# A written order on five engines for the last turn of a two-layer graph kernel, with the end by row blocks

## The chip, the cores and the metric

The kernel runs on one core of a Trainium2 chip. The metric is the device time of one execution in microseconds (us); the figure for a kernel is the median of several executions. The engines are TensorE (PE, matrix products), VectorE (DVE), ScalarE (ACT), GpSimd (POOL) and SyncE (SP, which issues the DMAs here).

## The reference

The input is 64 graphs of 256 nodes with 256 features, and a 0/1 adjacency matrix for each graph. Two layers follow each other, all in float32.

```
layer 0:  h = gat(gat(x, adj, W1, a1), adj, W2, a2)        # softmax over one axis of leaky_relu scores
          h = layernorm(x + h) * g_ln1 + b_ln1
          x = layernorm(h + relu(h @ w_ff1 + b_ff1) @ w_ff2 + b_ff2) * g_ln2 + b_ln2
layer 1:  q, k = x @ Wq + bq, x @ Wk + bk                  # 8 heads of 32
          attn = softmax(q k^T / sqrt(32))
          out  = sum over r of (attn * (adj == r)) @ (x @ Wv[r] + bv[r])     # adj has 0 and 1 only
          x    = layernorm(x + out @ Wo + bo) * g1 + beta1
          out  = layernorm(x + gelu(x @ W1 + b1) @ W2 + b2) * g2 + beta2
```

The hidden width of both feed-forward parts is 1024.

## The kernel before

**Tiling.** Two graphs (G = 2) are worked on together as a pair `u`. There are 32 pairs (NG). A pair's activations `y` are T = 4 row blocks of 128 rows by 256 features; the first NB = 2 blocks are graph 0 of the pair, the other two are graph 1. A layer norm takes, for each row block, statistics on DVE (`bn_stats`, `bn_aggr`, L842 and L843), the inverse deviation on POOL (`rs`, an add and a power, L853 and L854), an offset `nm` on DVE (`offsets`, L861), and one ACT instruction that applies both (`applied_norm`, L871). The gain and the shift of the norm come later as two DVE passes over all four blocks (`affine` = `times` L880 and `plus` L883, 128x1024 elements each). `rg2`/`rb2`, `rg3`/`rb3` and `rg4`/`rb4` are gain and shift of the second norm of layer 0 and of the two norms of layer 1.

**Stages.** A turn `turn(y_, x_, z)` (L1238) works on three pairs: the attention and the feed-forward part of layer 1 for pair `y_`, the feed-forward part of layer 0 for the next pair, and the attention layers of layer 0 for the pair after that. PE works through the stages without a gap in the middle of the run, since each stage's waits are covered by products of another pair. In turn 30 there is no third pair left, in turn 31 neither a second nor a third.

**The pieces of a turn's layer 1.** `Projections` computes queries, keys and values with seven half-size products each (steps q1 to q7 and v1 to v7). It reads the features transposed, with a row of ones that carries the bias; POOL writes that row (`with_ones`, memset L692). `scores(n)`, n = 0 to 3, are the products for one graph and one half of the heads, with their exponentials on ACT (`powers`); `masks(n)` multiplies by the adjacency and `totals(n)` sums pairs, both on DVE. `sums(n)` gives the weighted values (`po`) and the row sums (`zo`) on PE. `shares(b)` is a chain on DVE that divides graph b: transpose of `zo`, reciprocal, transpose, multiply (L1131, L1132, L1138, L1140). It empties the PSUM bank of `po`. `out_(b)` is the output projection `yop` and its addition to y (L827, L830).

**The feed-forward part.** `hidden_seven` (L885) gives the hidden layer with seven products in place of eight; step names are a digit and a half, "7a" for example, and the letters c, d and s stand for activations alone. Each product goes to a PSUM bank, which ACT copies (L927) or DVE adds (L924) into the hidden features. Four differences of the transposed features (L897) are made on DVE first. `HiddenOut` (L974) is the way back to 256 features, again with seven products, taken in the order 1, 2, 5, 6, 3, 7, 4. Products 1, 6, 7 and 4 share one bank, and 5 and 3 another; `add` (L1012) adds a product to one half of a graph's y, and `sums` (L990) forms the four sums of the hidden features.

**The order of the work.** The instructions are written in one Python program for all engines, and a scheduler in the framework arranges each engine's queue by its own priorities. Inside `tc.manual_schedule(engines=...)` the named engines keep the written order. The outer loop names PE and SP. A turn names PE, SP, DVE and ACT, but turn 31 names only PE and SP (`[:4 if X else 2]`), so its work on DVE, ACT and POOL is placed by the scheduler. A framework rule adds semaphore waits wherever one engine reads or overwrites what another still uses.

**Turns 30 and 31.** The feed-forward output of pair 30 is not done in its own turn. `out_pieces` (L1196) is a generator that holds its seven products, and `piece()` (L1234) lets turn 31 run the next one between its scores. `finish` (L1216) norms one graph, applies rg4 and rb4 and issues the store of that graph, 256 KB. In turn 31 the affine steps of pair 30 (rg3, rb3) and pair 31 (rg2, rb2) are done by DVE, from the list `late`. Pair 29's last affine step (rg4, rb4) and store lie in turn 30 (L1520 to L1522). The program ends with a check: sums of values gathered on the way (`low`, `lowg`, `high`, `other`), a one-column product, and the flag `bad` (L1711 to L1720), which SP loads and all engines branch on (L1729).

Of the kernel before, what the change touches and what calls it, by code (L numbers as in the profile page):

```python
# [385 lines left out]
def narrow_path(  # L386
# [498 lines left out]
    def hidden_seven(u, l, hT, w, bi, func, d, tt):  # L885
# [13 lines left out]
        sub(0, quarter[0][1], quarter[0][0])  # L899
        sub(1, quarter[1][1], moving(0))  # L900
        sub(2, quarter[1][1], quarter[0][1])
        sub(3, quarter[1][0], moving(1))
# [68 lines left out]

        return steps

    class HiddenOut:  # L974
# [17 lines left out]
        def product(s, n):  # L992
# [4 lines left out]
            for old, new in ((1, 6), (6, 7), (7, 4), (5, 3)):  # L997
                if n == new:
                    s.ps[n] = s.ps[old]
            a, w_ = {1: (s.a[0], b11), 2: (s.a[1], b21), 5: (s.s[0], t1), 6: (s.s[1], t2),  # L1000
                     3: (s.s[3], b22), 7: (s.s[2], t3), 4: (s.a[3], t4)}[n]
            for i in range(NB):
                for k in range(K2):
                    nc.tensor.matmul(s.ps[n][:, i * F2:(i + 1) * F2], a[:, k, i * P:(i + 1) * P], w_[:, k, :],  # L1004
                                     start=n in (1, 2, 5) and i == 0 and k == 0, stop=True,
                                     skip_group_check=True)

        def add(s, n):
            b, o = {1: (0, 0), 2: (0, 0), 5: (1, 1), 6: (0, 1), 3: (0, 1), 7: (1, 1), 4: (1, 0)}[n]
            F2 = F // 2  # L1010
            yq = s.y[:, b * NB:(b + 1) * NB, o * F2:(o + 1) * F2]
            mark["out"] = nc.vector.tensor_tensor(yq, s.ps[n][:, :F].rearrange("p (i f) -> p i f", i=NB), yq, ALU.add)  # L1012
# [183 lines left out]
    def out_pieces(u, y, h1):  # L1196

        if u == NG - 2:
            s = [io.tile([P, T, N], F32, tag="y", name=f"sq{u}", bufs=4),
                 work.tile([P, T, WX], F32, tag="wh", name=f"wq{u}")[:, :, :N]]  # L1200
            s += [io.tile([P, T, N], F32, tag=t, name=f"sq{u}_{t}", bufs=1) for t in ("xq", "aq")]
        else:
            s = out_sums(u, 1)
        end = HiddenOut(u, 1, y, h1, w2s, s)
        end.sums(1, 2, 4, 3)
        for n, p in enumerate((1, 2, 5, 6, 3, 7, 4)):
            end(p)
            if n in (4, 6):
                finish(u, y, n // 6)
            yield  # L1210
# [5 lines left out]
    def finish(u, y, b):  # L1216

        normed(u, 3, y, range(b * NB, (b + 1) * NB))
        bt = slice(b * NB, (b + 1) * NB)
        affine(y[:, bt, :], rg4, rb4)  # L1220
        stored(u, y, bt)
# [11 lines left out]

    def piece():  # L1234
        if left:
            next(left[0], None)

    def turn(y_, x_, z):  # L1238
# [43 lines left out]
        def moved(moves, n):  # L1282
            for _ in range(n):
                nc.scalar.copy(*next(moves))

        order = tc.manual_schedule(engines={getattr(mybir.EngineType, n) for n in
                                            ("PE", "SP", "DVE", "Activation")[:4 if X else 2]})
        with order:
# [29 lines left out]
            if X:  # L1318
# [58 lines left out]
                totals(3)  # L1377
                sums(2)
                sums(3)
                first("4b")  # L1380
            else:
                powers(0, (1,))
                p("q3 v3")
                powers(0, (2, 3))
                p("q6 v6 q7 v7")
                with behind("projected"):
                    masks(0)
                    totals(0)
                while late:
                    affine(*late.pop(0))  # L1390
                p("q4 v4")
                scores(1)
                masks(1)
                totals(1)
                sums(0)
                piece()
                scores(2)
                sums(1)
                piece()
                with behind("out"):  # L1400
                    shares(0)
                masks(2)
                totals(2)
                scores(3)
                piece()
                piece()
                masks(3)
                totals(3)
                sums(2)
                sums(3)  # L1410
# [13 lines left out]
            piece()  # L1424
# [9 lines left out]
            piece()  # L1434
# [21 lines left out]
            elif X:  # L1456
                out.product(5)
                out.sums(3)
                out.add(5)
            if X and not Z:  # L1460
                out(6)
# [11 lines left out]
            elif X:  # L1473
                out.sums(4)
                out(7, 3)
            if not Z:
                piece()
                hT = to_features(y, f"h3T{y_}")
                hT = [h.rearrange("p (t a r) -> p t a r", t=T, r=32) for h in hT]
                if not X:  # L1480
                    affine(y, rg3, rb3)
# [33 lines left out]
            else:  # L1515
# [4 lines left out]
                if waiting:  # L1520
                    affine(waiting[0][1], rg4, rb4)
                    stored(*waiting.pop(), slice(0, T))  # L1522
                if X:
                    offsets(*n)
                    applied_norm(X["y"], *n, [0])
                second("3a")
# [3 lines left out]
                if X:  # L1530
                    applied_norm(X["y"], *n, [2, 3], True)
                second("6a 6b ca cb da db 7a 7b")
# [3 lines left out]
            if y_ >= NG - 2:  # L1536
                pieces = out_pieces(y_, y, h1)
                if X:
                    left.append(pieces)
                    late.append((y, rg3, rb3))  # L1540
                    late.append((X["y"], rg2, rb2))
                else:
                    for _ in pieces:
                        pass
# [216 lines left out]
```

## Time and profile before

| what | us |
|---|---|
| median of 3 executions (all three alike) | 2962.51 |
| the profiled execution | 2958.02 |
| span in its profile | 2956.4 |
| PE busy | 2923.1 (99%) |
| DVE busy | 2607.3 (88%) |
| ACT busy | 1902.0 (64%) |
| POOL busy | 628.2 (21%) |

Times in the profile run from the start of the span. Turn 30's attention ends near 2838, turn 31's projections start at 2869.78, its last output products at 2931.34, and the span ends at 2956.4. A row of the timeline gives start, duration, engine, line, operation, the written and the read tiles with their shapes, a count if several are joined, and the idle time of that engine before it with what ended the wait. A row of the windows gives the stretch, its length, the busy time of PE, PEld, DVE, ACT and POOL with their instructions, the clock that PE was granted (1.00 is full), and the DMA figures.

### The profile page before, as it was taken

The page shows a single profiled execution, that of the slowest core. Times are in us where ns is not written, and L with a number is a line of the kernel's source. Part 1 is how long each engine was busy: PE and PEld are TensorE (multiplying, and loading weights), DVE is VectorE, ACT ScalarE, POOL GpSimd, SP SyncE. Part 2 cuts the span into 40 slices and gives each one's busy share as a digit, 9 for nine tenths or more (in the row PEclk, how much of TensorE's full clock was granted, in tenths as well). Part 3 has the DMA queues.
Part 4 walks back from the last instruction along what each step waited for, and adds up shares of the span by engine and source line. Part 5 has one row for each costly group of instructions (what it writes and reads, how often), then busy time and mean ns, then how long its engine had stood idle before and what let it go on. Part 6 is the DMA issues. An engine that isn't in the chain of part 4 may idle for free.

```text
span 2956.4 us, 58614 instructions
## 1 busy us (share of the span) xinstructions
PE 2923.1 (99%) x22192; PEld 2504.0 (85%) x22192; DVE 2607.3 (88%) x5023; ACT 1902.0 (64%) x3990; POOL 628.2 (21%) x930
## 2 busy tenths in 40 slices
PE   8999999999999999999999999999999999999998
PEld 6788888888888888888888888888888888888876
DVE  5788899889999888999889898989998889988987
ACT  5476676676666666766766666666667667667653
POOL 4222121122221221211221211221112212112211
PEclk9999999999999999999999999999999999999999
DMA  5011111111111111111111111111111111111000
GB/s 152 11 32 32 37 30 28 31 35 37 34 30 23 39 32 37 32 30 28 39 32 37 28 24 38 32 38 32 33 24 39 32 37 30 29 32 32 18 8 16
DMA packets 407955, 99.27 MB, mean 34 GB/s; under 512 B 357770, under 2 KB 407156, under 8 KB 407668
## 3 DMA queue, kind: packets, MB, share of 16 engines
q1 hardware_dynamic: 406268, 94.13, 14.7%
q8 instruction: 178, 2.92, 0.4%
q0 software_dynamic: 1056, 1.05, 0.1%
q14 instruction: 109, 0.89, 0.1%
q10 hardware_dynamic: 344, 0.28, 0.0%
HBM read 56.78 MB, written 16.78 MB: 25 GB/s over the span
## 4 chain that ended last, share of the span: by engine, by line
PE 96%; DVE 2%; ACT 1%; POOL 1%; issue 0%; DMA 0%; ACTq 0%; POOLq 0%; DVEq 0%
PE yf L1004 26%; PE h1a L915 15%; PE h1b L915 11%; PE po L1120 8%; PE qk L1071 6%; PE v L1071 6%; PE sp L1092 4%; PE hpp L816 4%; PE xpp L755 4%; PE yop L827 4%; PE ygp L827 4%; PE zo L1123 2%; PE rows L764 1%; ACT y L871 0%; DVE st L842 0%
## 5 line engine op out<-in xcount | busy, mean ns | idle before, releaser
L1101 ACT ACTIVATE e<-sp 128x512 f32<-128x512 f32 x512 | 271.1, 612 | 71.2 <-issue 43.8
L1105 DVE TENSOR_TENSOR ea<-e,aT 128x1024 f32<-128x1024 f32 x256 | 310.2, 1213 | 1.6 <-ACT e L1101 1.6
L871 ACT ACTIVATE y<-y,nm,rs 128x256 f32<-128x256 f32 x450 | 239.5, 591 | 84.4 <-DVE nm L861 79.4
L924 DVE TENSOR_TENSOR h<-h1a,h 128x512 f32<-128x512 f32 x293 | 197.0, 680 | 83.7 <-PE h1a L915 80.9
L927 ACT COPY h<-h1b 128x512 f32<-128x512 f32 x293 | 175.3, 599 | 124.3 <-PE h1b L915 122.5
L933 ACT ACTIVATE h<-h,cols 128x256 f32<-128x256 f32 x512 | 221.9, 502 | 35.8 <-DVE h L924 31.6
L717 POOL COPY hT<-yt 32x256 f32<-32x256 f32 x244 | 211.2, 866 | 146.5 <-DVE yt L700 135.4
L1058 ACT COPY qk<-qk 128x512 f32<-128x512 f32 x128 | 74.3, 581 | 240.7 <-PE qk L1071 240.0
L853 POOL TENSOR_SCALAR rs<-mv 128x4 f32<-128x4 f32 (+1 forms) x134 | 42.7, 319 | 813.7 <-DVE mv L843 440.2
L1012 DVE TENSOR_TENSOR y<-yf,y 128x256 f32<-128x256 f32 x448 | 184.9, 413 | 34.3 <-PE yf L1004 34.2
L842 DVE BATCH_NORM_STATS2 st<-y 128x6 f32<-128x256 f32 x512 | 208.5, 408 | 5.6
L933 ACT ACTIVATE h<-h1a,cols 128x256 f32<-128x256 f32 x256 | 102.5, 465 | 132.0 <-PE h1a L915 132.0
L1133 POOL TENSOR_TENSOR low<-low,rq 128x16 f32<-128x16 f32 x64 | 13.9, 217 | 813.1 <-DVE rq L1132 813.1
L883 DVE TENSOR_TENSOR y<-y,rb 128x1024 f32<-128x1024 f32 (+1 forms) x130 | 166.1, 1278 | 2.3
L880 DVE TENSOR_TENSOR y<-y,rg 128x1024 f32<-128x1024 f32 (+1 forms) x130 | 155.6, 1197 | 1.2 <-ACT y L871 1.1
L1110 DVE TENSOR_TENSOR es<-e 128x1024 f32<-128x1024 f32 x128 | 155.4, 1214 | 0.0
L854 POOL TENSOR_TENSOR rs<-rs,mhalf 128x4 f32<-128x4 f32 (+1 forms) x134 | 139.8, 1044 | 8.4
L1092 PE MATMUL sp<-qk 32*128 32x256 f32 x2048 | 137.9, 394 | 0.0
L915 PE MATMUL h1a<-tt,wf 128*128 128x256 f32 x512 | 137.7, 392 | 0.0
L1120 PE MATMUL po<-e,v 128*32 128x256 f32 x2048 | 135.5, 382 | 0.0
L1120 PE MATMUL po<-ea,v 128*32 128x256 f32 x2048 | 134.4, 379 | 0.0
L700 DVE STREAM_TRANSPOSE yt<-y 128x256 f32<-128x256 f32 x364 | 128.1, 407 | 0.6 <-ACT y L871 0.6
(280 smaller groups left out, 7721.0 us busy)
## 6 DMA issues: line engine op xcount, KB each, us to landing
hT<-yt SPq DMA_DIRECT2D x666, 32.0 KB, 1.9
y<-in_x_dram SPq DMA_DIRECT2D x32, 512.0 KB, 4.8
xq<-in_x_dram SPq DMA_DIRECT2D x240, 64.0 KB, 2.2
aq<-in_adj_dram SPq DMA_DIRECT2D x240, 64.0 KB, 2.4
out_dram<-y SPq DMA_DIRECT2D x30, 512.0 KB
wf<-in_L_gnn_w_ff_dram SPq DMA_DIRECT2D x2, 1024.0 KB, 7.2
w<-in_L_gnn_W_dram SPq DMA_DIRECT2D x2, 1024.0 KB, 8.2
first<-in_adj_dram POOLq DMA_DIRECT2D x2, 512.0 KB, 7.9
```

The lines of the kernel that those rows point to most:

```text
L717: nc.gpsimd.tensor_copy(to, at)
L827: nc.tensor.matmul(ps[:, i * F:(i + 1) * F], lhs(t, k), rhs(b, k), start=(k == 0), stop=(k == n - 1))
L842: nc.vector.bn_stats(st[:, t, :], y[:, t, :])
L871: mark["normed"] = nc.scalar.activation(y[:, t, :], y[:, t, :], AF.Identity, bias=nm[:, t:t + 1], scale=rs[:, t:t + 1])
L915: nc.tensor.matmul(ps[:, i * N:(i + 1) * N], w_[:, f * P:(f + 1) * P], m, start=first and i == 0, stop=True, skip_group_check=True)
L933: nc.scalar.activation(y, y if ps is None else ps[:, i * N:(i + 1) * N], func, bias=bi[:, f:f + 1])
L1004: nc.tensor.matmul(s.ps[n][:, i * F2:(i + 1) * F2], a[:, k, i * P:(i + 1) * P], w_[:, k, :], start=n in (1, 2, 5) and i == 0 and k == 0, s ...
L1071: nc.tensor.matmul(ps[:, i * N:(i + 1) * N], l, r, start=n in (1, 2, 5) and i == 0, stop=True, skip_group_check=True)
L1092: nc.tensor.matmul(ps[a][:, j * N:(j + 1) * N], k_[hp, m, j0:j0 + P], q[hp, m, b * N:(b + 1) * N], start=True, stop=True)
L1101: nc.scalar.activation(e[:, a, :], ps[a], AF.Exp, scale=isd)
L1105: nc.vector.tensor_tensor(ea[:, a:a + 2, :], e[:, a:a + 2, :], ab[:, None, :].to_broadcast([P, 2, NB * N]), ALU.mult)
L1120: nc.tensor.matmul(po[hp, m * N:(m + 1) * N], vs[:, hp], w[:, a, j * N:(j + 1) * N], start=(n == 0), stop=(n == len(terms) - 1))
```

## The change

Turn 31 gets a block of its own, with PE, SP, DVE, ACT and POOL all in written order. Pair 30's left-over output products stand by name between the scores of pair 31. In turn 30, step 4b moves ahead of `sums(2)` and `sums(3)`, and the second layer's sums are taken in the order 4, 3 around product 6. Pair 29's last multiply (rg4) stays in turn 30; its addition (rb4) and its store move to turn 31. Pair 30's affine step rg3/rb3 moves into turn 30 and from DVE to POOL; pair 31's rg2/rb2 moves to POOL; pair 31's rg3/rb3 stays on DVE. The last norm works by row block: statistics, then `(y - mean) * rg4` as one DVE instruction, and later `* rs + rb4` as another, with a store of 128 KB per block, in place of the ACT apply and two DVE passes per graph. The order in which finishing and products stand for pair 30 is by graph; the last feed-forward output cuts products 7 and 4 in halves by row block. The differences of the last hidden layer (`subs`) are taken later, after step 1b, and pair 31's last transposed features come graph by graph.

```diff
-    def hidden_seven(u, l, hT, w, bi, func, d, tt):
+    def hidden_seven(u, l, hT, w, bi, func, d, tt, subs=True):
...
+        def differences():
+            sub(0, quarter[0][1], quarter[0][0])
...
+        if subs:
+            differences()
...
-        def product(s, n):
+        def product(s, n, blocks=range(NB)):
...
-        def add(s, n):
+        def add(s, n, i0=0, i1=NB):
...
-    def out_pieces(u, y, h1):
...
+    def last_out(u, y, h1):
+
+        end = HiddenOut(u, 1, y, h1, w2s, out_sums(u, 1))
+        end.sums(1, 2, 4, 3)
+        end(1, 2, 5, 6, 3)
+        n = finish(u, y, range(NB))
+        end.product(7, [0])
+        end.add(7, 0, 1)
+        end.product(7, [1])
+        finished(u, y, *n[0])
+        end.add(7, 1, 2)
+        end.product(4, [0])
+        finished(u, y, *n[1])
+        end.add(4, 0, 1)
+        n = finish(u, y, range(NB, NB + 1))
+        end.product(4, [1])
+        end.add(4, 1, 2)
+        n += finish(u, y, range(NB + 1, T))
+        for m in n:
+            finished(u, y, *m)
...
-        normed(u, 3, y, range(b * NB, (b + 1) * NB))
-        bt = slice(b * NB, (b + 1) * NB)
-        affine(y[:, bt, :], rg4, rb4)
-        stored(u, y, bt)
+    def finish(u, y, blocks):
+
+        n = []
+        for t in blocks:
+            at = ((u - NG + 2) * T + t) * 16
+            st, mv, rs = (g["fin"][:, 0, at + a_:at + b_] for a_, b_ in ((0, 6), (6, 8), (8, 9)))
+            nc.vector.bn_stats(st, y[:, t, :])
+            nc.vector.bn_aggr(mv, st)
+            nc.gpsimd.tensor_scalar(rs, mv[:, 1:2], EPS, 0.0, op0=ALU.add, op1=ALU.add)
+            nc.gpsimd.tensor_tensor(rs, rs, mhalf[:, 0:1], ALU.pow)
+            nc.gpsimd.tensor_add(high[:, t:t + 1], high[:, t:t + 1], mv[:, 0:1])
+            nc.vector.scalar_tensor_tensor(y[:, t, :], y[:, t, :], mv[:, 0:1], rg4,
+                                           op0=ALU.subtract, op1=ALU.mult)
+            n.append((t, rs))
+        return n
+
+    def finished(u, y, t, rs):
+        nc.vector.scalar_tensor_tensor(y[:, t, :], y[:, t, :], rs, rb4, op0=ALU.mult, op1=ALU.add)
+        nc.sync.dma_start(out[G * u + t // NB, t % NB * P:(t % NB + 1) * P, :], y[:, t, :])
...
+        if X is None:
+            with tc.manual_schedule(engines={getattr(mybir.EngineType, n) for n in
+                                             ("PE", "SP", "DVE", "Activation", "Pool")}):
...
+                p.sums()
+                nc.scalar.activation(work.tile([P, 1], F32, tag="ve", name=f"ve{y_}_0"), mhalf[:, 0:1], AF.Exp)
+                p("q2 v2 q1 v1 q5 v5")
+                for w, wy in waiting:
+                    plus(wy, rb4)
+                    stored(w, wy, slice(0, T))
+                nc.gpsimd.tensor_mul(y, y, rg2[:, None, :].to_broadcast([P, T, F]))
+                nc.gpsimd.tensor_add(y, y, rb2[:, None, :].to_broadcast([P, T, F]))
+                p("q6 v6")
+                end.sums(1)
+                p("q3 q7 v7")
+                end.sums(2, 4)
+                p("v3 q4 v4")
+                end.sums(3)
+                scores(0)
+                scores(1, ())
+                end.product(1)
+                powers(1, range(HPB))
+                masks(0)
+                end.add(1)
+                end.product(2)
+                totals(0)
+                end.add(2)
+                end.product(5)
+                masks(1)
+                end.add(5)
+                totals(1)
+                scores(2, ())
+                sums(0)
+                powers(2, range(HPB))
+                sums(1)
+                masks(2)
+                scores(3)
+                end.product(6)
+                totals(2)
+                end.add(6)
+                shares(0)
+                masks(3)
+                totals(3)
+                sums(2)
+                sums(3)
+                out_(0)
+                end(3)
+                shares(1)
+                last = finish(u, yu, range(NB))
+                n0 = norm(y_, 2, y, range(NB))
+                out_(1)
+                end.product(7)
+                offsets(*n0)
+                applied_norm(y, *n0, range(NB))
+                n1 = norm(y_, 2, y, range(NB, T))
+                end.add(7)
+                ph = turned(y, f"h3T{y_}", range(NB))
+                end.product(4)
+                offsets(*n1)
+                applied_norm(y, *n1, range(NB, T))
+                nc.scalar.activation(work.tile([P, 1], F32, tag="ve", name=f"ve{y_}"), mhalf[:, 0:1], AF.Gelu)
...
+                end.add(4)
+                for m in last:
+                    finished(u, yu, *m)
...
+                second("2a 1a")
+                turned(y, f"h3T{y_}", range(NB, T), ph)
...
+                second("2b 1b")
+                second.subs()
+                last = finish(u, yu, range(NB, T))
+                affine(y, rg3, rb3)
+                second("5a 5b 3a 3b 6a 6b ca cb da db")
+                for m in last:
+                    finished(u, yu, *m)
+                second("7a 7b sa sb 4a 4b")
+                last_out(y_, y, h1)
+            return
...
+                if not Z:
+                    first("4b")
                 sums(2)
                 sums(3)
-                first("4b")
...
+                if Z:
+                    first("4b")
...
                 out.product(5)
-                out.sums(3)
+                out.sums(4)
                 out.add(5)
-            if X and not Z:
-                out(6)
+                out.product(6)
...
-                out.sums(4)
-                out(7, 3)
+                out.add(6)
+                out.sums(3)
+                out(3, 7)
...
-                if waiting:
-                    affine(waiting[0][1], rg4, rb4)
-                    stored(*waiting.pop(), slice(0, T))
...
+                times(waiting[0][1], rg4)
                 second("3a")
...
+                nc.gpsimd.tensor_mul(y, y, rg3[:, None, :].to_broadcast([P, T, F]))
+                nc.gpsimd.tensor_add(y, y, rb3[:, None, :].to_broadcast([P, T, F]))
                 second("6a 6b ca cb da db 7a 7b")
...
-                    late.append((y, rg3, rb3))
-                    late.append((X["y"], rg2, rb2))
...
+            if not Z:
+                left.append((y_, y, h1))
                 return
```

## The prediction

> **What bounds the kernel now.** I read the shares of busy time on the page first, then the critical chain, then the windows of 20 us over the last two turns, and then the timelines of PE, DVE and POOL where a window shows PE below 20.
>
> ```profile
> PE 2923.1 (99%) x22192; PEld 2504.0 (85%) x22192; DVE 2607.3 (88%) x5023; ACT 1902.0 (64%) x3990; POOL 628.2 (21%) x930
> PE 96%; DVE 2%; ACT 1%; POOL 1%; issue 0%; DMA 0%; ACTq 0%; POOLq 0%; DVEq 0%
> 2860.00:2880.00 20.00, 16.39 (x80) 12.73 (x79) 15.08 (x21) 14.93 (x31) 1.61 (x3) 0.91 0.08 27
> 2900.00:2920.00 20.00, 18.07 (x173) 14.58 (x172) 16.23 (x38) 4.13 (x8) 4.95 (x11) 1.00 0.04 14
> ```
>
> PE is the bound, and the chain is 96% PE. The two window rows (length, then PE, PEld, DVE, ACT and POOL busy, then the clock) show where that fails: 3.6 and 1.9 us of PE's time are lost, once with the clock at 0.91. The instructions of both programs stand in the same order until the last scores of turn 30 (2829 us), so only the last 127 us can move. The one exception is the load of the Exp table for turn 31, which the scheduler pulls up into turn 29's ACT queue, where it costs two more table loads beside an idle ACT: 0 to 0.5 us, taken as 0.
>
> ```profile
> 2861.62 0.15 DVE L861 SCALAR_TENSOR_TENSOR nm<-mv,rs 128x4 f32<-128x4 f32 x1
> 2863.66 3.47 PE L915 MATMUL h1a<-tt,w 128*128 128x256 f32 x8 [1.96 <-DVE h L924]
> 2869.21 0.52 POOL L692 MEMSET h2T<- 1x512 f32 x1 [6.23 <-issue]
> 2869.78 1.03 PE L1071 MATMUL qk<-h2T,wqk 128*128 128x256 f32 x4
> 2906.01 0.72 DVE L1131 STREAM_TRANSPOSE rz<-zo 128x512 f32<-128x512 f32 x1 [1.47 <-PE zo L1123]
> 2906.76 0.25 DVE L1132 RECIPROCAL rq<-rz 128x16 f32<-128x16 f32 x1
> 2907.05 0.71 DVE L1138 STREAM_TRANSPOSE rz<-rq 128x512 f32<-128x512 f32 x1
> 2907.79 0.69 DVE L1140 TENSOR_TENSOR qk<-po,rz 128x512 f32<-128x512 f32 x1
> 2949.48 0.15 DVE L1720 TENSOR_SCALAR bad<-goodp 1x1 int32<-1x1 f32 x1 [0.37 <-PE goodp L1719]
> 2950.61 0.69 DVE L883 TENSOR_TENSOR y<-y,rb 128x512 f32<-128x512 f32 x1
> ```
>
> Columns are start, duration, engine, line, operation, and in brackets the idle time before and its releaser. The offsets nm came behind two affine passes of DVE, and PE stood 1.96 us at 7a; its next eight products took 3.47 instead of the 1.73 of two such steps. The shares of a graph are a chain of four DVE instructions, 2.5 us long. The end hangs on the flag `bad` and the last store.
>
> [...]
>
> ```profile
> 2844.25 1.19 DVE L990 TENSOR_TENSOR eaq<-h 128x1024 f32<-128x1024 f32 x1
> 2844.49 1.03 POOL L853 TENSOR_SCALAR rs<-mv 128x2 f32<-128x2 f32 x1 [3.45 <-DVE mv L843]
> L616 POOL TENSOR_TENSOR w2t<-w,w2t 128x512 f32<-128x512 f32 x2 | 2.5, 1272 | 0.1
> L616 POOL TENSOR_TENSOR wvs<-wvs,wv 128x256 f32<-128x256 f32 x1 | 0.7, 726 | 0.1
> ```
>
> POOL's tiny instruction takes 1.03 under such a DVE pass and 0.23 elsewhere. So POOL's new passes must be priced with collisions. [...] Here a wait of only 1.96 brought the half clock, and one of 1.46 (2943.68) showed nothing comparable. The forecast goes by the trace: a wait of 2 us or more may cost about 1.7 more.
>
> **The change part by part**, as the distance of after from before at PE's place, in us.
>
> (1) *Turn 30, 4b ahead of sums(2).* 4b needs the bank that DVE's add for 7b reads (2830.67 to 2831.35, behind masks). Before, the po and zo products of two quads stood between; now PE waits from 2828.84 to 2831.39, 2.5 us. The sums, which lost some 0.7 to `ea` and `es`, find them ready. +1.8; 0.2 returns until step 2a: +1.6.
>
> (2) *Turn 30, second hidden layer.* DVE's passes over y30 with rg3 and rb3 (1.22 + 1.23) go to POOL, and y29's with rb4 go to turn 31, so nm is no longer behind them: the 1.96 and the 1.6 of half clock go. But POOL runs its two passes ahead of what follows. A 128x1024 pass is shown nowhere; from 0.73 and 1.27 the line gives 2.35, doubling 2.54. I take 2.35 and 0.4 for collisions. POOL is free near 2858, nm is at 2860.4, the transposes of h2T end at 2866.07 and 4b at 2867.7, against 2869.78 before. -3.7, together -2.1.
>
> (3) *Turn 31's start: POOL's queue.* y31's multiply by rg2 and addition of rb2 now also stand on POOL, and ahead of the memset (L692) of the ones row that q2 reads. They wait for the transposes at 2866.07, which read the same y. 2866.07 + 2 x 2.35 + 0.4 + 0.52 + hops gives q2 at 2871.85 instead of 2869.78. Only 4a and 4b (1.73) cover it, so PE stands 4.15 us. +2.1. [...]
>
> (4) *Projections and scores.* The DVE passes of y30 and y31 that held PE at 2874.49 (1.10) and 2879.18 (0.55) are gone. Fourteen steps of 0.867 (12.1), four scores (4.3), four half-width output products of 1.785 (7.1), two blocks of po and zo (4.5), changes of shape (0.4), and about 1.7 where the second scores wait for the exponentials behind the Exp table load (ACT, 1.28): PE comes to quad 2's po at 2871.85 + 30.1 = 2901.95, against 2901.41 before. +0.55.
>
> (5) *shares(0).* On DVE, add(6) stands ahead of shares(0), and waits for product 6, which is PE's last work before po of quad 2; po needs the bank that shares(0) empties. So 0.34 for the add and 0.72 + 0.28 + 0.74 + 0.69 for the chain, with hops, lie open: po starts at 2904.85, 2.9 us later. Before, this chain lay beside scores and two output products. +3.45 at yop of graph 0 (2909.3 against 2905.87).
>
> (6) *shares(1).* The same with yop0's add and add(3) ahead of it: yop of graph 1 comes at 2915.95, against 2909.48, where yop0 and product 3 (3.6) hid the chain. A stall of 3.0; +6.5.
>
> (7) *Norm, transposes and second hidden layer of turn 31.* Finishing y30 by row (bn_stats to aggregate 0.46, a fused pass about 0.42 for each block) stands on DVE between: PE waits about 1.9 for the normalised first half, 0.9 for ACT's copy behind the Gelu load (1.28), 1.24 at 5a for tt, 0.8 at 7a behind L880/L883 of y31. That is 4.8 against 2.0 before (0.95, 0.16, 0.78, 0.16), and about 0.7 fewer changes of shape. The last layer's first output product starts at 2939.87 against 2931.34. +8.5.
>
> (8) *The end by row blocks.* ACT's apply and two 0.69 passes become two fused passes of 0.42 per row, and four stores become eight of 128 KB on SP, where they wait in line with y29's; each is 0.38 of issue. But 7 and 4 are cut in half products (0.89), of which three wait for the preceding half's add, and these adds stand behind bn_stats, aggregate and fused passes of the other rows. Five products reach 2948.8; add(3) and two blocks' statistics bring 7's second half to 2951.4, 4's halves start at 2952.7 and about 2954, and the last fused pass ends near 2958. `bad`, which before was done ahead of the last pass, now follows POOL's last sum into `high`: 2959.5. From `bad` to the span's end took 6.9 (2949.48 to 2956.4), from the store's issue 5.0 (2951.37). By `bad`: 2966.3; were the store what counts, 2963.2. I take the first. +9.9.
>
> Four waits are new and above 2 us: (1), (3), (5), (6). Each may start a half-clock window worth up to 1.7: 0 to 7; I take one or two, 1.7 to 2.
>
> **Sum.** 1.6 - 3.7 + 4.2 - 1.55 + 2.9 + 3.0 + 2.05 + 1.4 = 9.9, and 1.7 for the clock: 11.6. The profiled execution took 2958.02 (span 2956.4 and 1.6 around it), the median shown is 2962.51, 4.5 above it; I add the difference to the median: 2974. A change is told from none here by about 0.2%, 5.9 us.
>
> **The rivals.**
> *A, DVE is what binds, and relieving it pays (0.09).* Place: DVE from 2850 on. If the waits of (3), (5) and (6) do not reach PE, the gains are left: 1.96, 1.6, 1.1, 0.55 and some 2 at the end, -7: 2955.5. For it: nearly every wait of PE in this stretch before has DVE as its releaser. Against it: the chain starts only when zo or product 6 is there, however idle DVE is. It decides at po of quad 2: the shares must be divided by 2901.9, so must start by 2899.4, before product 6 ends.
> *B, the waits are partly covered (0.15).* The fixed order costs (1) and (3), but POOL's passes are cheap (q2 at 2870.6), the end follows the store (-3.2), (7) is no worse than before (-2.1), and the clock holds: +3.5, 2966. For it: my starts in (7) are stacked on each other.
> *C, the clock falls at each long wait (0.22).* +9.9 and 7 or so, with q2 at 2873.4: 2981. For it: 1.96 us was enough at 2863.66. Against: 1.46 was not[...].
> *That the change doesn't do what it says:* the Exp load ahead of the projections is moved to turn 29, as told, and the load still falls before the first exponential; this is inside the forecast.
>
> **How the numbers follow.** The forecast has 0.54 and its own range is 2969 to 2978 (POOL's passes -1.2 to +1.5, the store -3.2, the clock 0 to +3.4). The range for 8 in 10 leaves out A and the top of C: 2962 to 2981. Slower by over 0.2% (above 2968.4): the forecast, C, and none of B: 0.76. Within: B, 0.15. Faster: A, 0.09.
>
> **What would show it.** In the changed profile: a wait of about 2.5 at 4b near 2831; none at 7a near 2862 and a full clock there; POOL passes of 128x1024 of 2.3 to 2.6 and the memset behind them, with PE idle about 4 before the first qk; waits of about 3 at po near 2905 and at the second yop near 2916; and `bad` behind the last pass of DVE, within 7 us of the end. POOL passes below 1.7, or the shares ahead of add(6), would make it wrong by several us; a clock at 1.00 throughout takes 2 off, at 0.9 in several windows adds 5.

## The result and the profile after

The changed kernel takes 2980.99 us (median of 4 runs, 2978.15 to 2982.18) against 2962.51 beside it: +18.5 us. The ratio measured over the runs is 1.0066, with a 95% interval of 1.0054 to 1.0078; that of the two medians is 1.0062. The forecast was 2974, +11.5, with a range of its own of 2969 to 2978.

The profiled execution has a span of 2980.5, 24.1 more than the one before. Matching PE's products one by one shows that 4.8 of this is already there at turn 29 (near 2710 us), where both programs are written the same. Of these, 4.3 come from the first 100 us, where the mean clock was 0.91 in this profile and 0.93 in the one before. The last two turns are worth **+19.3 us in this pair of profiles**.

The waits of PE from 2780 us to the end of the changed kernel (engine, line, what released it; the sum, how often, the longest):

```profile
PE qk L1077 <- POOL h2T L692: 3.9, 1, 3.9
PE h1a L919 <- DVE h L928: 3.7, 3, 2.3
PE goodp L1790 <- DVE good L1788: 3.6, 1, 3.6
PE po L1126 <- DVE qk L1146: 3.0, 1, 3.0
PE yop L827 <- DVE qk L1146: 3.0, 1, 3.0
PE yf L1009 <- DVE y L1017: 2.9, 3, 2.1
PE h1b L919 <- DVE tt L897: 1.3, 1, 1.3
PE sp L1098 <- ACT e L1107: 1.1, 1, 1.1
PE h1a L919 <- ACT h3T L1374: 0.9, 1, 0.9
```

The four waits of the forecast are the longest, but for that of the closing check's product `goodp`, which stands behind all other products and was there before (3.5). Their rows in PE's timeline, with 7a of turn 30 between:

```profile
2836.64 1.13 PE L919 MATMUL h1a<-tt,wf 128*128 128x256 f32 x4 [2.33 <-DVE h L928]
2870.93 2.10 PE L919 MATMUL h1a<-tt,w 128*128 128x256 f32 x8 [0.68 <-DVE h L928]
2879.56 2.08 PE L1077 MATMUL qk<-h2T,wqk 128*128 128x256 f32 x4 [3.93 <-POOL h2T L692]
2881.43 1.91 PE L1077 MATMUL v<-wv,h2T 128*128 128x256 f32 x4
2889.45 1.03 PE L1077 MATMUL qk<-h2T,wqks 128*128 128x256 f32 x4
2917.75 1.07 PE L1126 MATMUL po<-e,v 128*32 128x256 f32 x16 [2.99 <-DVE qk L1146]
2928.97 2.96 PE L827 MATMUL yop<-wo,qk 128*128 128x256 f32 x8 [2.99 <-DVE qk L1146]
```

The wait of 1.96 at 7a is down to 0.68, as meant. But the step behind the wait of 3.93 takes 2.08 and 1.91 instead of the usual 1.03, and the yop behind the last wait 2.96 instead of 1.89: the clock's record has 0.50 there, from 2878.60 to 2885.42 and from 2929.80 to 2933.21. The stretches of that record last 3.41 us or a multiple of it in this profile (10.24, 6.83, 3.41 and so on; only the last is cut short by the end). The windows of the changed kernel on that grid (start and end, length, busy PE, its weight loads PEld, DVE, ACT and POOL, then the clock and the DMA figures) show what goes ahead of a switch:

```profile
2834.22:2837.64 3.42, 1.09 (x5) 0.68 (x4) 3.42 (x6) 2.24 (x4) 0.00 (x0) 1.00 0.00 0
2837.64:2841.05 3.41, 3.41 (x33) 1.55 (x36) 1.21 (x2) 0.84 (x2) 0.00 (x0) 0.50 0.00 0
2875.18:2878.60 3.42, 0.45 (x3) 0.05 (x1) 1.54 (x1) 3.42 (x10) 3.34 (x2) 1.00 0.00 0
2878.60:2882.01 3.41, 2.45 (x6) 2.01 (x7) 1.10 (x3) 0.51 (x2) 0.85 (x2) 0.50 0.00 0
2882.01:2885.42 3.41, 3.41 (x10) 2.70 (x9) 0.27 (x1) 0.83 (x2) 0.00 (x0) 0.50 0.00 0
2895.66:2899.08 3.42, 2.33 (x21) 1.33 (x18) 2.70 (x4) 3.41 (x6) 0.00 (x0) 1.00 0.00 0
2899.08:2902.49 3.41, 3.41 (x17) 3.41 (x18) 1.13 (x1) 1.67 (x4) 0.00 (x0) 0.50 0.00 0
2912.73:2916.14 3.41, 2.03 (x20) 1.84 (x16) 1.55 (x4) 2.06 (x4) 0.00 (x0) 1.00 0.01 2
2916.14:2919.56 3.42, 1.81 (x36) 1.37 (x40) 3.35 (x4) 0.00 (x0) 0.22 (x1) 1.00 0.02 5
2926.38:2929.80 3.42, 0.83 (x4) 0.78 (x5) 3.25 (x8) 0.00 (x0) 0.55 (x2) 1.00 0.00 0
2929.80:2933.21 3.41, 3.41 (x13) 2.94 (x12) 2.72 (x9) 0.00 (x0) 3.03 (x8) 0.50 0.00 0
```

Behind the windows in which PE was busy for 1.09, 0.45 and 0.83 us, the clock was 0.50 in the next one. The wait of 2.99 ahead of po straddles two windows and leaves PE busy for 2.03 and 1.81 us of them; the clock stayed 1.00, and the po products behind it took 1.07. The window from 2895.66 had 2.33 busy, more than these two, and 0.50 came behind it; the products in it are scores of 32 rows (`sp<-qk`, 32x256). The clock's record has six half-clock windows between 2800 and the end of the last output product, the sixth from 2967.34; the kernel before has one there, from 2864.01.

The passes on POOL take what was estimated (2.35), and stand ahead of the memset:

```profile
2874.08 2.36 POOL L1321 TENSOR_TENSOR y<-y,rg 128x1024 f32<-128x1024 f32 x1 [2.93 <-PE h2T31p L532]
2876.51 2.41 POOL L1322 TENSOR_TENSOR y<-y,rb 128x1024 f32<-128x1024 f32 x1
2878.99 0.52 POOL L692 MEMSET h2T<- 1x512 f32 x1
```

And the chain of shares on DVE starts only behind the add for product 6, which waits for PE:

```profile
2914.80 0.42 DVE L1017 TENSOR_TENSOR y<-yf,y 128x256 f32<-128x256 f32 x1 [1.82 <-PE yf L1009]
2915.14 0.71 DVE L1137 STREAM_TRANSPOSE rz<-zo 128x512 f32<-128x512 f32 x1
2916.92 0.69 DVE L1146 TENSOR_TENSOR qk<-po,rz 128x512 f32<-128x512 f32 x1
```

### The profile page after: what moved, and what is told of

Read it like the earlier page. It is cut to its first block, busy times and chain, and to the rows that moved or that the text cites. A ratio compares the mean times of both kernels' runs of the same rounds, so it can differ in the third digit from the quotient of the medians.

```text
span 2980.5 us, 58636 instructions
## 1 busy us (share of the span) xinstructions
PE 2935.4 (98%) x22192; PEld 2514.0 (84%) x22192; DVE 2611.9 (88%) x5026; ACT 1902.3 (64%) x3987; POOL 646.9 (22%) x946
## 4 chain that ended last, share of the span: by engine, by line
PE 96%; DVE 2%; POOL 1%; ACT 1%; issue 0%; DMA 0%; ACTq 0%; POOLq 0%; DVEq 0%
PE yf L1009 26%; PE h1a L919 15%; PE h1b L919 11%; PE po L1126 8%; PE qk L1077 6%; PE v L1077 6%; PE sp L1098 4%; PE hpp L816 4%; PE xpp L755 4%; PE ygp L827 4%; PE yop L827 4%; PE zo L1129 2%; PE rows L764 1%; DVE st L842 0%; ACT y L871 0%
## 5 line engine op out<-in xcount | busy, mean ns | idle before, releaser
L1017 DVE TENSOR_TENSOR y<-yf,y 128x256 f32<-128x256 f32 (+1 forms) x450 | 186.0, 413 | 41.8 <-PE yf L1009 41.6
L883 DVE TENSOR_TENSOR y<-y,rb 128x1024 f32<-128x1024 f32 x124 | 161.1, 1300 | 2.2
L880 DVE TENSOR_TENSOR y<-y,rg 128x1024 f32<-128x1024 f32 x124 | 150.6, 1215 | 0.0
L1098 PEld LDWEIGHTS sp<-qk 32*128 32x128 f32 x2048 | 96.1, 184 | 39.4 <-issue 31.2
```

What stands on the lines that cost most here:

```text
L1098: nc.tensor.matmul(ps[a][:, j * N:(j + 1) * N], k_[hp, m, j0:j0 + P], q[hp, m, b * N:(b + 1) * N], start=True, stop=True)
```

## The experiments

Two theories. **Waits and clock**: the time is the sum of the waits that the written order opens and of the half-clock windows that they bring. **Waits alone**: the half clock falls where PE would have stood anyway. A third, rival A of the forecast, says that a fixed order with less work on DVE can win. Times are compared as a distance from the kernel before in the same session, where its median was 2962.58 in the first group of runs, 2961.95 in the second, 2960.44 in the third and 2962.71 in the last.

| kernel | median | from before |
|---|---|---|
| changed, first and second time | 2980.99, 2980.42 | +18.5, +18.5 |
| shares ahead of the adds | 2974.89 | +12.3 |
| memset ahead of POOL's passes | 2977.44 | +14.9 |
| 4b behind the sums | 2976.55 | +14.0 |
| the three together | 2965.66 | +5.2 |
| changed, waits filled, too long | 2984.70 | +22.1 |
| changed, waits filled | 2975.35 | +13.4 |
| changed, end by graph | 2980.28 | +19.8 |
| before, pair 29's affine moved | 2958.16 | -3.8 |
| new order, first, second, third | 2965.31, 2962.40, 2957.77 | +3.4, +2.0, -4.9 |

**The shares.**

```diff
                 end.product(6)
+                shares(0)
                 totals(2)
                 end.add(6)
-                shares(0)
...
                 sums(3)
+                shares(1)
                 out_(0)
                 end(3)
-                shares(1)
```

> The changed kernel with one order undone on DVE: the shares of graph 0 go ahead of the totals of quad 2 and of the add for product 6, the shares of graph 1 directly behind the sums of quad 3. Theory (waits and the clock): both waits of 2.99 us go (po near 2917.8, second yop near 2929), and with the second the half-clock window at 2929.6 that cost 1.7: 6 to 8 us faster than the changed kernel, 2973 to 2975. Rival (DVE is full, so the waits only move): less than 3 us, with new PE waits behind DVE in the same stretch.

Measured: 6.2 us faster than the changed kernel, as the first theory had it. Both waits of 2.99 are gone. But one came in the place of the second, in PE's timeline of this run:

```profile
2924.69 1.39 PE L516 MATMUL h3T31p<-ident,y 128*128 128x128 f32 x4 [2.32 <-ACT y L871]
```

The normalised half of pair 31 had been late all along, behind DVE's finishing of pair 30; the second wait for the shares and the half clock behind it had hidden it.

**POOL's queue.** The multiply is made to wait for the memset.

```diff
-        nc.gpsimd.memset(hT[KB - 1][one], 1.0)
+        mark["ones"] = nc.gpsimd.memset(hT[KB - 1][one], 1.0)
...
-                nc.gpsimd.tensor_mul(y, y, rg2[:, None, :].to_broadcast([P, T, F]))
+                with behind("ones"):
+                    nc.gpsimd.tensor_mul(y, y, rg2[:, None, :].to_broadcast([P, T, F]))
```

> The changed kernel with POOL's multiply by rg2 and addition of rb2 for pair 31 placed behind the memset of the ones row. Theory: PE's wait of 3.93 us ahead of the first qk goes, and with it the two half-clock windows behind it (3.4 us): 6 to 8 us faster, 2973 to 2975. Rival (the tq differences on DVE or the copies of h2T are as late as the memset): at most 1.5 us of the wait goes, and some 3 of time.

Measured: 3.6 us faster in the medians, less than expected; with four runs each, the two ranges overlap (2975.63 to 2979.92 against 2978.15 to 2982.18). The wait of 3.93 at the first qk is gone (0.41 is left at q5), but the two half-clock windows came back elsewhere. What follows came earlier, and rows behind waits of the same length grew. The po behind its 2.99 took 1.94 in place of 1.07; the second scores and the output product behind them took 2.37 and 6.33 in place of 1.61 and 5.47, one half-clock window more; and the yop took 3.39 in place of 2.96:

```profile
2909.45 1.94 PE L1126 MATMUL po<-e,v 128*32 128x256 f32 x16 [2.99 <-DVE qk L1146]
2921.94 3.39 PE L827 MATMUL yop<-wo,qk 128*128 128x256 f32 x8 [2.99 <-DVE qk L1146]
```

**4b.** The step goes back behind the sums.

```diff
-                if not Z:
-                    first("4b")
                 sums(2)
                 sums(3)
-                if Z:
-                    first("4b")
+                first("4b")
```

> The changed kernel with step 4b of turn 30 back behind the sums of quads 2 and 3. Theory: PE's wait of 2.33 at 4b and the half-clock window behind it (1.7) go, and waits of 0.7 for ea and es come back: 2.5 to 3.5 us faster. If the clock plays no part: 1.6.

Measured: 4.5 us faster, more than expected. At turn 30's output products PE is 3.4 us ahead, as the theory had it; the rest comes from further on, where this profile has three half-clock windows in place of six (their rows: 2.08 and 1.58 at the first qk and v, 2.80 and 2.82 at the second yop and the product behind it, 1.56 and 2.08 at the halves of product 4). One of the three that are missing is the one behind 4b; whether the other two are more than the luck of where the windows fell is not shown.

**The three together.** All three diffs above in one kernel.

> The changed kernel with three orders undone together: shares ahead of the adds, POOL's rg2/rb2 behind the memset, 4b behind the sums. The single runs gave 6.1, 3.5 and 4.4 us, 14.0 together. If the parts add up: 2966 to 2968. If the wait of 2.3 for the normalised half, which the second of the shares uncovered, and its half-clock window stay as they are: the same. If less time in front of a wait only lengthens the next: over 2970.

Measured: 13.3 us faster than the changed kernel, against 14.3 as the sum of the single runs. Within the scatter they add up; the wait for the normalised half is there (2.31).

**The clock by itself.** PE is given products to do while it waits, with rb4 as an operand, which is zero in this data; they go to a bank that is started anew, or add zero. Nothing that PE waits for becomes ready earlier.

```diff
+    def fill(ps, n, start=False):
+        for _ in range(n):
+            nc.tensor.matmul(ps[:, 0:N], rb4[:, 0:P], wo[:, 0, :], start=start, stop=True,
+                             skip_group_check=True)
...
+                fill(end.ps[5], 13)
                 sums(2)
```

> The changed kernel with all its waits, but PE is kept busy in four of them by products of 0.217 us with a zero operand (rb4 is zero in this data): 10 ahead of 4b in turn 30, 17 ahead of the first qk, 13 ahead of po of quad 2, 13 ahead of the second yop. Nothing that follows becomes ready earlier. Theory (the clock doubles the price of long waits): the half-clock windows at 2837, 2878 to 2885, 2930, and perhaps 2899, do not come, 5 to 8 us faster than the changed kernel: 2973 to 2976. Rival (the waits alone are the loss, the half clock falls where PE would have waited anyway): within 1 us of the changed kernel, or slower where the added products run over.

Measured: 3.6 us slower than the changed kernel. I had mis-read the price: a row with x4 for two products gives 0.433 us for one, not 0.217. So the fillings ran over by 10 x 0.433 - 2.33 = 2.0, 17 x 0.433 - 3.93 = 3.4, and twice 13 x 0.433 - 2.99 = 2.6, 10.7 in all. That the time rose by 3.6 only already says that some 7 us came back. With half as many (`fill(end.ps[5], 6)` and so on):

> As the run with added products, but with half as many, since each took 0.433 us there and they ran past the waits: 5 ahead of 4b (2.2 of 2.33 us), 8 ahead of the first qk (3.5 of 3.93), 6 ahead of po (2.6 of 2.99), 6 ahead of the second yop (2.6 of 2.99). The waits are as long as before, only busy. Theory (the clock): four or five half-clock windows of 1.7 us do not come: 5 to 8 us faster than the changed kernel. Rival (waits alone): within 1 us.

Measured: 5.1 us faster than the changed kernel in the medians. Of the changed kernel's nine runs one (2973.55) lies inside the range of these five (2969.37 to 2976.36), the other eight above it. In the profile the waits are as long as before, filled: here the 2.33 at 4b and the 3.93 at the first qk.

```profile
2828.76 2.32 PE L1206 MATMUL po<-wo,rb 128*128 128x256 f32 x10
2831.25 1.13 PE L919 MATMUL h1a<-tt,wf 128*128 128x256 f32 x4 [0.17 <-DVE h L928]
2868.43 3.62 PE L1206 MATMUL qk<-wo,rb 128*128 128x256 f32 x16
2872.53 1.13 PE L1079 MATMUL qk<-h2T,wqk 128*128 128x256 f32 x4 [0.49 <-POOL h2T L692]
```

The windows of this run up to the last products (first fence) against those of the changed kernel, taken again (second):

```profile
2820.00:2860.00 40.00, 39.68 (x330) 33.12 (x321) 30.78 (x53) 14.12 (x28) 8.70 (x8) 1.00 0.01 1
2860.00:2900.00 40.00, 37.76 (x287) 30.43 (x286) 29.57 (x38) 22.05 (x43) 8.58 (x7) 1.00 0.04 14
2900.00:2940.00 40.00, 34.77 (x261) 27.90 (x257) 28.05 (x63) 13.20 (x27) 9.08 (x18) 1.00 0.03 10
```

```profile
2820.00:2860.00 40.00, 37.52 (x354) 29.06 (x353) 29.34 (x45) 16.90 (x34) 3.94 (x6) 0.96 0.01 1
2860.00:2900.00 40.00, 34.31 (x173) 28.06 (x172) 28.29 (x41) 21.10 (x42) 13.34 (x9) 0.91 0.04 14
2900.00:2940.00 40.00, 33.05 (x330) 26.98 (x330) 26.33 (x51) 9.66 (x19) 4.75 (x12) 0.92 0.02 8
```

Clock 1.00 throughout in one, 0.91 to 0.96 in the other, at waits of the same length; only one of 1.3 us for the normalised half comes into sight in the filled kernel. Measured from turn 29 on, the filled kernel's profile is 11.9 us longer than that of the kernel before, and the changed kernel's first one 19.3. So in these profiles about **12 of 19.3 are waits and 7.4 are the clock**. "Waits alone" falls. The 7.4 are an upper figure: the profiled execution is the fastest of the five, and caught no half-clock window in its last two turns (clock 1.00 from 2820 to 2956); the medians have 5.1, and the others' mean clocks of 0.994 and 0.995 against its 0.997 suggest, without a profile to show it, that they kept some. The clock's part is thus about 5 to 7.4.

**The changed kernel again.**

> The changed kernel once more, for its scatter: 2978 to 2983, waits of the same length as in the first profile, the half-clock windows in part in other places. If the 4 us by which it runs behind already in the first 100 us belong to the program, they are there again; if they come from where the clock's windows fall, they differ from profile to profile.

Measured: 2980.42 (2973.55 to 2982.54), the same +18.5. Over all profiles of this study the distance at turn 29 from the kernel before runs from -0.5 to +5.0 us. In the first 100 us, where all programs are the same, the mean clock was 0.91 in the changed kernel's first profile, 0.93 in the one before and 0.95 in the one with the waits filled: five, four and three half-clock windows. Of the 4.8 us, the 4.3 from the first 100 us are thus not the program's. The other 0.5 gathers evenly between 100 and 2700 us in all nine profiles of the changed order (0.4 to 0.6) and hardly in those of the other four kernels (at most 0.1); its cause is open.

**The end.** Products 7 and 4 whole, ACT's apply and two affine passes per graph, two stores.

```diff
         end(1, 2, 5, 6, 3)
-        n = finish(u, y, range(NB))
-        end.product(7, [0])
...
+        n = norm(u, 3, y, range(NB))
+        end(7)
+        end.product(4)
+        applied_norm(y, *n)
+        end.add(4)
+        affine(y[:, 0:NB, :], rg4, rb4)
...
```

> The changed kernel with the end by graph again: products 7 and 4 whole, the adds for 7 and 4 ahead of the affine passes, ACT's apply and two stores of 256 KB. Theory: the waits of 2.10, 0.38 and 0.38 shrink to about 1 in all, and the half-clock window at 2967 may go: 1.5 to 4 us faster than the changed kernel. Rival (the row blocks pay by an earlier last store): 0 to 2 us slower.

Measured: +19.8 from before against +18.5, while its profile is 1.6 shorter from turn 29 on, and its waits at the output products fell from 2.10, 0.38 and 0.38 to 0.52, while the closing check's product waits 5.1 in place of 3.6. The two readings disagree in sign, and only 5 runs stand behind the median: whether the end by row blocks costs or gains is open; the two readings are some 1.5 us either way.

**One part of the change alone, on the kernel before.** Pair 29's multiply goes behind the offsets of turn 30, its shift and store behind the add for 7b.

```diff
-                if waiting:
-                    affine(waiting[0][1], rg4, rb4)
-                    stored(*waiting.pop(), slice(0, T))
                 if X:
                     offsets(*n)
                     applied_norm(X["y"], *n, [0])
+                if waiting:
+                    times(waiting[0][1], rg4)
...
+                if waiting:
+                    plus(waiting[0][1], rb4)
+                    stored(*waiting.pop(), slice(0, T))
```

> The kernel before with one part of the change alone: pair 29's multiply (rg4) behind the offsets of turn 30 instead of ahead of them, its shift and store behind the add for 7b. Theory: the wait of 1.96 at 7a and the half-clock window behind it (1.6) go: 3 to 4 us faster than before. Rival (another wait takes its place, for h2T's copies behind the shift): 0 to 1.5 us.

Measured: 3.8 us faster than before (ratio 0.9989, interval 0.9982 to 0.9995). The wait of 1.96 is gone (0.2 is left), and the eight products behind it, in the second row, take 2.10 in place of 3.47:

```profile
2861.52 1.89 PE L915 MATMUL h1a<-tt,w1s 128*128 128x256 f32 x8
2863.43 2.10 PE L915 MATMUL h1a<-tt,w 128*128 128x256 f32 x8
```

So this part of the change pays by itself about what step (2) of the forecast had for it, 3.7.

**A written order that wins.** The first attempt undoes the three orders, lets pair 31's norm go ahead of pair 30's finishing, moves pair 29's multiply and pair 31's shift behind the adds for 7b, leaves out the Exp load, and ends with whole products.

```diff
-                last = finish(u, yu, range(NB))
                 n0 = norm(y_, 2, y, range(NB))
...
                 end.add(7)
+                last = finish(u, yu, range(NB))
...
-        end(1, 2, 5, 6, 3)
+        end(1, 2, 5, 6)
+        end.product(3)
+        end.product(7)
+        end.add(3)
+        end.add(7)
+        end.product(4)
         n = finish(u, y, range(NB))
```

> A version meant to beat both: the changed kernel with the shares ahead of the adds, POOL's rg2/rb2 behind the memset, 4b behind the sums, the norm of pair 31 ahead of the finish of pair 30 on DVE, pair 29's multiply and pair 31's shift behind the adds for 7b, no Exp load of its own, and the last output's adds for 3 and 7 ahead of the statistics of graph 0, whole products at the end. Theory: the waits of 2.33, 3.93, 2.99, 2.99 and 2.1 and their half-clock windows go, 0.7 comes back at 4b's sums and about 1 ahead of the transposes: 20 to 23 us faster than the changed kernel, 2958 to 2961, and 2 to 4 under the kernel before. Rival (the fixed order as such is slow, work in the last turn is bounded by DVE): 2966 to 2972.

Measured: +3.4. The second yop starts at 2908.73 against 2909.48 in the kernel before, though this profile runs 0.6 late at turn 29, so PE is 1.4 us ahead there; the transposes and the end give it back: 0.50, 1.42 (ACT's copy behind the Gelu load) with a half-clock window at it (the products behind it take 1.58 in place of 1.13, the next transposes 1.06 in place of 0.60), and 1.28, then the last add behind fused passes that wait for POOL. DVE's rows show one cost more, beside POOL's row (in the changed kernel too: there such differences take 2.46 in turn 30 and 1.85 in turn 31):

```profile
2868.59 2.59 POOL L1318 TENSOR_TENSOR y<-y,rg 128x1024 f32<-128x1024 f32 x1
2868.88 2.58 DVE L1045 TENSOR_TENSOR tq<-h2T 128x256 f32<-128x256 f32 x1
```

The second attempt, against the first:

```diff
-                with behind("ones"):
-                    nc.gpsimd.tensor_mul(y, y, rg2[:, None, :].to_broadcast([P, T, F]))
-                nc.gpsimd.tensor_add(y, y, rb2[:, None, :].to_broadcast([P, T, F]))
...
                 end.sums(3)
+                affine(y, rg2, rb2)
...
+                views = [h.rearrange("p (t a r) -> p t a r", t=T, r=32) for h in to_features(y, f"h3T{y_}")]
...
+                second("2a 1a 2b 1b")
+                last = finish(u, yu, range(NB))
+                second("5a 5b")
```

> From the run meant to beat both, with what its trace left: the transposes of the last hidden layer all at once as in the kernel before and the Gelu load behind their copies (waits of 0.50, 1.42 and 1.28 and a half-clock window of 1.7 there), pair 31's rg2/rb2 back on DVE behind the sums (POOL's passes held the tq differences for 2.6 us each), pair 29's multiply behind the tq differences (a wait of 1.14 for the memset), and the last add for product 4 ahead of the fused passes that wait for POOL. Theory (the fixed order can gain what the kernel before lost at 7a, in the projections and at the last product): 2956 to 2959, 3 to 6 us under the kernel before. Rival (DVE's work has to wait somewhere): 2961 to 2964.

Measured: +2.0, inside the rival's range. All the waits named are gone, the same difference takes DVE 0.42, but the finishing of pair 30 now stood between the hidden layer's adds:

```profile
2931.15 6.54 PE L919 MATMUL h1a<-tt,w 128*128 128x256 f32 x16 [3.11 <-DVE h L928]
```

The third places pair 30's four blocks one by one where DVE is idle: one ahead of the add for its product 4, one behind the adds for 1a and 1b, two between the last output's adds.

```diff
+                last = finish(u, yu, range(1))
                 end.add(4)
...
                 second("2a 1a 2b 1b")
-                last = finish(u, yu, range(NB))
+                last += finish(u, yu, range(1, NB))
...
         end(1, 2, 5, 6)
+        last = finish(w, wy, range(NB, NB + 1))
         end.product(3)
         end.product(7)
         end.add(3)
+        last += finish(w, wy, range(NB + 1, T))
         end.add(7)
```

> From the second attempt to beat both: pair 30's graph is no longer finished between the hidden layer's adds, where it made PE wait 3.11 us at 7a with two half-clock windows (3.4); one block stands beside the norm of pair 31, one behind the adds for 1a and 1b, two between the last output's adds. Theory: the 3.1 and the 3.4 go and no wait over 1.7 us is left ahead of the end: 2955 to 2958, 3 to 6 us under the kernel before. Rival (the four blocks cost DVE time wherever they stand): no wait of its own but a later end, 2959 to 2961.

Measured: 2957.77 against 2962.71, ratio 0.9984, interval 0.9976 to 0.9992. The waits of PE in its last two turns are

```profile
PE goodp L1776 <- DVE good L1774: 6.0, 1, 6.0
PE yf L1009 <- DVE y L1017: 1.4, 2, 0.9
PE sp L1098 <- ACT e L1107: 1.1, 1, 1.1
PE h1b L919 <- DVE h3T L533: 0.8, 1, 0.8
PE h1a L919 <- DVE h L928: 0.7, 1, 0.7
PE yf L1009 <- DVE eaq L995: 0.2, 1, 0.2
```

and, but for the closing check's at the end, none of them brought a half-clock window (clock 1.00 from 2820 to 2946). PE's last output product comes 4.9 us earlier, counted from turn 29, and the end behind it gives 1.4 back. A fixed order on five engines is thus not slow as such. What it adds is not shown: this kernel also has pair 29's passes out of the way of the offsets, which alone gave 3.8, and the two intervals (0.9976 to 0.9992 and 0.9982 to 0.9995) overlap.

## Why the prediction was right or wrong

The direction, the places and, in the main, the causes were right; one term of the sum was mis-sized above all: **the clock**, put at 1.7 us and measured at 5 to 7.4. The waits came to 11.9 where the forecast had 9.9. By the steps of the forecast:

- (1), (3), (5), (6): waits of 2.5, 4.15, 2.9 and 3.0 were forecast, and 2.33, 3.93, 2.99 and 2.99 measured, each with the releaser named. Undoing the orders took 13.3 of the 18.5 us away: this is shown for the three orders together, their half-clock windows included.
- (2) was too good by 0.7: a multiply of pair 29 is still on DVE ahead of the adds (7a waits 0.68). I had also called the passes ahead of the offsets pair 30's. They were pair 29's, as the run that moves these alone shows.
- (4) had 1.7 for the second scores; measured 1.09. The Exp load in turn 29's queue took 0.4, inside the 0 to 0.5.
- (7) named four waits; 0.90, 1.28 and 0.69 of them are there. The first, 1.9 for the normalised half, is hidden by the wait and the half clock ahead of it; it shows as 1.3 in the run with the waits filled and as 2.32 where the shares come early.
- (8) had the end 1.4 longer. From the start of the last output products it is 27.2 against 25.1, 2.1 longer, with one half-clock window in it.
- The waits together, counted from turn 29 and with a full clock, come to 11.9. The forecast had 9.9 ahead of the clock; 0.7 of the difference is (2) and 0.4 the Exp load.
- The clock term, the step that failed: "one or two" windows, 1.7. Measured: six windows, and 7.4 us against the profile with the waits filled, 5.1 in the medians. The estimate of up to 1.7 for one window stands (7.4 over six is 1.2 each); the number of windows was wrong. I counted long waits and gave each a small chance. In this profile three of the four forecast waits left PE idle for 2.33, 2.96 and 2.59 us of one window of 3.41 and brought the half clock, the longest for two windows; the fourth left 1.38 and 1.61 in two windows and brought none. A wait of 1.09 beside 32-row products and one of 2.10 at the end (1.83 idle in its window) brought one window each.

Rival C, "the clock falls at each long wait", put 2981 and 0.22 on this; it was nearly the case, save that one wait straddled two windows and shorter waits took its place. Rival A fell for this order. With the shares early enough a fixed order did win, by 4.9 us, but that relieving DVE as such pays is not shown: that kernel has pair 31's rg2 and rb2 back on DVE, and moving pair 29's passes gave 3.8 by itself.

## What to carry over

In this kernel, price a new wait of PE by its length plus, as an estimate from the half-clock stretches of 3.41 us (7.4 us over six measured), up to 1.7 us for each one that it may bring: waits that left PE idle for 1.83 to 2.96 us of one window brought one or two, a wait of 2.99 split into 1.38 and 1.61 over two windows brought none, and 1.09 us beside products of 32 rows brought one. In a written order, look for each instruction that waits for the engine it is about to serve, such as an add for the product just issued, and put the chains that empty a bank ahead of it. When a wait is removed, the next one behind it may have been hidden there: undo orders singly and together before adding up their gains.

## What the runs showed of the hardware

- In the last two turns, on the grid of the clock's record and leaving out the drop behind PE's last output product, the changed kernel's first profile had 0.50 behind the full-clock windows with PE idle for 2.33, 2.96, 2.59 and 1.83 us of 3.41, and behind one with 1.09 idle and score products of 32 rows; the clock stayed 1.00 behind those with 1.38, 1.61 and 1.28 idle. In the kernel before it was 0.50 behind 1.96 and stayed 1.00 behind 0.95, 0.97 and 1.36. In the first 100 us it also fell behind windows with 0.33 and 0.00 idle (changed) and 0.32 and 0.00 (before); why is open.
- Behind the wait of 1.09 and the 32-row scores, the output product took 5.27 to 6.33 us in six profiles and 3.84 in five; why not in all is open.
- The half-clock stretches of identical stages begin at other times: the first at 25.05 us in the changed kernel's first profile and at 24.12 in the one before. In the first 100 us the clock was 0.50 in five windows and in four of these two, and the profiles were up to 5.5 us apart at turn 29; the scatter of the kernel before is a little wider (2956.77 to 2964.25 in 41 runs).
- POOL's pass of 128x1024 takes 2.36 to 2.41 us in the changed kernel, and 2.59 in the first new order, where a difference `tq` on DVE had begun just ahead of it (2868.54, 0.43 long). The next such difference, beside that pass, takes 2.58 instead of 0.42, and ends 0.28 behind it. In these rows DVE takes longer as well as POOL; the forecast had priced this on POOL only.
